# A graph network layer: gathered rows as float16 high and low parts that TensorE adds to the products, and 47 double groups, not 18, fetched row by row

## The chip, the cores and the metric

The kernel runs on one core of one Trainium2 chip. That core has five engines with a queue of instructions each: TensorE (PE in the profile, its weight loads PEld), VectorE (DVE), ScalarE (ACT), GpSimd (POOL) and SyncE (SP). The queues run in order and wait for each other only through semaphores. The metric is the device time of one execution in microseconds (us). Before the change it is 3845.28 us, the median of three runs (3842.6 to 3846.54).

## What is computed

One layer of message passing over 12500 nodes with 128 features and 400000 edges, sorted by their target `dst`. Cut to what matters:

```
h   = relu(layernorm(x))                          # 12500 x 128
m   = relu(concat(h[src], h[dst], ea) @ w1 + b1) @ w2 + b2      # 400000 edges
agg = segment_sum(m, dst)
gi, gh = agg @ w_ih + b_ih, h @ w_hh + b_hh        # GRU gates
r, z = sigmoid(i_r + h_r), sigmoid(i_z + h_z);  n = tanh(i_n + r * h_n)
out = x + (1 - z) * n + z * h
```

`w1` has three parts: 128 rows for the source node, 128 for the target, 32 for the edge's own attributes. So the term of the source is a row of A = h @ w1[0:128], which is computed once per node and then fetched once per edge. Those 400000 fetches of 512 bytes, at addresses that only `src` tells, are what this change is about.

## The kernel before

**Tiling.** The edges make 3125 tiles of 128. Eight tiles are a double group (a pair k, 391 of them, the first with fewer tiles), and a pair is worked on in two halves u = 2k and 2k + 1 of four tiles (782 halves). The edges of a pair have targets in a short window of nodes. A tile has its edges on the 128 partitions; in a half, the four tiles lie beside each other, 128 x 512 numbers.

**Prologue.** The nodes are loaded in 25 chunks of up to four tiles; layer norm; a transpose on PE into `hT_all`, which holds h for all nodes with the features on the partitions and stays in SBUF; then A = h @ w1a, copied out of PSUM into `asb` by ScalarE in every fourth chunk and by VectorE in the others (L304), and written to DRAM. POOL begins to gather at once: the first ten pairs (`RAW`) take rows of x, not of A, and are normalised and multiplied tile by tile.

**A pair in the main loop.** `gather` (L135 to L146) issues eight indirect DMAs on POOL, one per tile, into a buffer G. There are two rings: eight buffers (`GBUFS`), and four more (`EARLY`) for the first pairs, which are closed later to make room for the jobs below. `fetch` (L483, L486) loads the edge attributes and the targets of two pairs into L and Ld over SP; L has three buffers. `onehot_T` (L493, VectorE) makes the upper rows of L a one-hot matrix of the target within the window, `onehot` (L542) the same with edges on the partitions. `window` (L512, L515) copies the window's columns of `hT_all` and multiplies them by w1b on PE; `window_rows` (L524) adds b1 and puts the result into RW over the attribute's part of w1. With that, one matmul of L by RW (L590) gives the sum of the target's and the attribute's terms for two tiles.

**A half.** `pre` (L586 to L602) issues two such matmuls into a PSUM tile (two of these exist); `add` (L605 to L615, VectorE) adds the gathered rows of A, from PSUM and G into G; `relu` (L617 to L623, ScalarE) writes the result to RB; `seg` (L625 to L636, PE) multiplies the one-hot matrix by it and so sums the edges per target. After a pair `take` copies the sums out (`sums` on VectorE, `dcol` on ScalarE). After every 14 pairs `node` computes the gates for the finished nodes, one step of it per half, spread over the queues.

**Pairs fetched by hand.** Some pairs don't use POOL. `one_by_one` (L762 to L781) loads 32 indices at a time into registers (L768) and then moves, edge by edge, a column of `hT_all` into a tile HE, as four bytes per partition: ScalarE with a copy (L775), VectorE with a maximum over one element (L777). Such a pair has 1024 edges. HE holds columns of h, so in `pre` PE multiplies each of its eight tiles by w1a into the same PSUM tile (L601), there is nothing to add, and `relu` reads PSUM. Ten pairs go to ScalarE and eight to VectorE (`SPREAD`), at even distances. A job is cut into steps of four edges (`STEP`), and `run_jobs` spreads its steps over the halves between the previous job's end and four halves before its pair is due, in four phases per half.

**The order.** It is written out by hand. In half u, phase 0 of the jobs comes first, then `take` of the pair before, then `stages(u)` (one-hots for three pairs ahead, `pre` for half u + 3, `add` and `relu` for u + 2), phase 1 and `window`, phase 2, `seg(u)`, phase 3 and `window_rows`, and a step of the node work. `JOBS0` (16) is the pair at which the jobs begin.

Of the kernel before, what the change touches and what calls it, by code (L numbers as in the profile page):

```python
# [37 lines left out]
NFULL = N // 128  # L38
BAT = (4,) + (8,) * 11 + (NFULL - 92, 1)
RAW = 10  # L40
GBUFS = 8
EARLY = 4
PLACE = 20
CH = PLACE * PAIR
LOAD = 32
STEP = {"act": 4, "dve": 4}
SPREAD = {"act": 10, "dve": 8}
NR = 12672

H_AT = 16512  # L50
HOLD = -2


@with_exitstack
def tile_gnn(ctx: ExitStack, tc: tile.TileContext, x, src, srcT, dstT, dstP, eaT, eaP, w1, b1, w2T, b2,
# [50 lines left out]
    def dst_tile(c):  # L106
        if c >= NPL:
# [4 lines left out]

    ident = const.tile([128, 128], F32, name="ident")
    make_identity(nc, ident)
    iota = const.tile([128, V], F16, name="iota")
    nc.gpsimd.iota(iota, pattern=[[1, V]], base=0, channel_multiplier=0,
                   allow_small_or_imprecise_dtypes=True)
    A = dram.tile([N, D], F32, name="A")
    stats = dram.tile([N, 2], F32, name="stats")
    S = dram.tile([NR, D + 1], F32, name="S")  # L120

# [13 lines left out]
    def gather(k):  # L135
        if k >= NP or k in mode:
            return
        pool = ge if early_pair(k) else gp
        G[k] = pool.tile([128, GRP, 2, D], F32, name="G")
        table = x if k < RAW else A  # L140
        for u in (2 * k, 2 * k + 1):
            for t, j, a in unit_tiles(u):
                c, i = divmod(t, CH)
                nc.gpsimd.indirect_dma_start(  # L144
                    out=G[k][:, j, a, :], out_offset=None, in_=table,
                    in_offset=bass.IndirectOffsetOnAxis(ap=src_i[c][:, i:i + 1], axis=0))  # L146

    for k in range(RAW):
# [59 lines left out]
    with tc.tile_pool(name="pp", bufs=3) as pp:  # L208
# [69 lines left out]
        def chunk(q):  # L278
            b, c = chunks[q]
            i0, n = bats[b]  # L280
            return b, i0, c, min(n, c + 4), PB(b), (i0 + c) * 128
# [3 lines left out]
        for q in range(NC + 3):  # L285
            if q < NC:
                b, i0, c, e, P, n0 = chunk(q)
                if c == 0:
                    stat(b + 2)
                    fin(b + 1)  # L290
            if 1 <= q <= NC:
                b, i0, c, e, P, n0 = chunk(q - 1)
                pts[q - 1] = ps2.tile([128, 512], F32, name="oh")
                for j in range(c, e):
                    nc.tensor.transpose(pts[q - 1][:, (j - c) * P:(j - c + 1) * P],
                                        xs[b][:P, j, :], ident[:P, :P])
                if e == bats[b][1]:
                    load(b + 5)
            if q >= 3:
                b, i0, c, e, P, n0 = chunk(q - 3)  # L300
                if c == 0:
                    asb[b] = pp.tile([128, 8, D], F32, name="asb", bufs=2)
                copy = nc.scalar.copy if q % 4 == 2 else nc.vector.tensor_copy
                copy(asb[b][:P, c:e, :], pas.pop(q - 3)[:P, :e - c, :])  # L304
            if q < NC:
                b, i0, c, e, P, n0 = chunk(q)
                for j in range(c, e):
                    relu_norm(xs[b][:P, j, :], xs[b][:P, j, :], st_all[:P, i0 + j, :])
                if e == bats[b][1]:
                    sqr(b + 2)  # L310
            if 1 <= q <= NC:
                b, i0, c, e, P, n0 = chunk(q - 1)
                copy = nc.scalar.copy if q % 4 == 0 else nc.vector.tensor_copy
                copy(columns(b, c, e), pts.pop(q - 1)[:, :(e - c) * P].rearrange(
                    "f (i p) -> f i p", i=e - c))
            if q >= 3:
                b, i0, c, e, P, n0 = chunk(q - 3)
                if e == bats[b][1]:
                    nc.sync.dma_start(nodes(A, i0, e, P), asb[b][:P, :e, :])
            if 2 <= q <= NC + 1:  # L320
                b, i0, c, e, P, n0 = chunk(q - 2)
                pas[q - 2] = ps2.tile([128, GRP, D], F32, name="pre")
                for j in range(c, e):
                    nc.tensor.matmul(pas[q - 2][:P, j - c, :], columns(b, j, j + 1)[:, 0, :],
                                     w1a, start=True, stop=True)
# [145 lines left out]
        nc.vector.tensor_copy(flag, f[:, 6:7])  # L471


    Ls, Ds, OH, RT, HE, SEG = ({} for _ in range(6))
    hand = {}

    def fetch(q):
# [104 lines left out]
    def pre(u):  # L582
        if u >= NU:
            return
        k, h = divmod(u, 2)
        PP[u] = ps2.tile([128, GRP, D], F32, name="pre")  # L586
        for i in range(2):
            c0 = (k % QP) * 512 + (2 * h + i) * 128
            raw = u in HE or k in hand
            nc.tensor.matmul(PP[u][:, 2 * i:2 * i + 2, :], Ls[k // QP][:, c0:c0 + 128], RW[k % 4],  # L590
                             start=True, stop=not raw)
            if raw:
                l = unit_tiles(u)
                for n, (t, j, a) in enumerate(l):
                    if j % 2 == i:
                        if k in hand:
                            c = (a * GRP + j) * 128
                            cols = hand[k][:, c:c + 128]
                        else:
                            cols = HE[u][:, n * 128:(n + 1) * 128]  # L600
                        nc.tensor.matmul(PP[u][:, 2 * i + a, :], cols, w1a, start=False,  # L601
                                         stop=n + 1 == len(l) or l[n + 1][1] != j)  # L602


    def add(u):  # L605
        if u >= NU:
            return
        if u in HE or u // 2 in hand:
            RT[u] = PP.pop(u)
            HE.pop(u, None)  # L610
            if u % 2:
                hand.pop(u // 2, None)
        else:
            RT[u] = unit(u)
            nc.vector.tensor_tensor(RT[u], PP.pop(u), RT[u], op=ALU.add)  # L615

    def relu(u):  # L617
        if u >= NU:
            return
        o = RB[u % 3]  # L620
        nc.scalar.activation(o[:, :, :D], RT.pop(u), AF.Relu)  # L621
        if u % 2:
            G.pop(u // 2, None)  # L623

    def seg(u):  # L625
        k, h = divmod(u, 2)
# [123 lines left out]

    pj = []
    late = ExitStack()
    by_hand = order["act"] + order["dve"]
    NJ = len(by_hand)
    at = const.tile([NJ, PAIR * 128], I32, name="at")

    def job_indices(r):
# [2 lines left out]
            "(o e) -> o e", o=1))  # L760

    def one_by_one(m, k):  # L762
        et = {"act": ET.Activation, "dve": ET.DVE}[m]
        r = by_hand.index(k)
        hand[k] = pj[0].tile([128, PAIR * 128], F32, name=f"HE_{m}")
        he = hand[k].bitcast(U8)
        for e0 in range(0, PAIR * 128, LOAD):
            _, vals = nc.values_load_multi_w_load_instructions(  # L768
                at[r:r + 1, e0:e0 + LOAD], engines=[et], min_val=H_AT,
                max_val=H_AT + 4 * (N - 1),  # L770
                skip_runtime_bounds_check_because="src holds numbers of nodes")
            for i, v in enumerate(vals):
                e = e0 + i
                if m == "act":
                    nc.scalar.copy(he[:, e * 4:e * 4 + 4], h_bytes[:, bass.ds(v - H_AT, 4)])  # L775
                else:
                    nc.vector.tensor_reduce(he[:, e * 4:e * 4 + 4],  # L777
                                            h_bytes[:, bass.ds(v - H_AT, 4), None],
                                            AX.X, ALU.max)
                if i % STEP[m] == STEP[m] - 1:  # L780
                    yield  # L781

# [2 lines left out]
    for m, kl in order.items():  # L785
        start = 2 * JOBS0
        for k in kl:
            end = 2 * k - 4
            jobs.setdefault(start, []).append((m, k, end - start))
            start = end  # L790
    live = {}

    PH = 4
# [37 lines left out]
    def stages(u):  # L831
        if u + 7 >= 0:
            raw_stats(u + 7)
        if u + 6 >= 0:
            raw_fin(u + 6)
            raw_h(u + 6)
        if u % 2 == 0:
            onehot_T(u // 2 + 3)
            onehot(u // 2 + 3)
        if u + 4 >= 0:  # L840
            raw_turn(u + 4)
        if u + 3 >= 0:
            pre(u + 3)
        if u + 2 >= 0:
            add(u + 2)
            relu(u + 2)

    for u in range(-7, 0):
# [13 lines left out]
    for u in range(NU):  # L862
# [14 lines left out]
        for r in range(2 * u, min(2 * u + 2, NJ)):  # L877
            job_indices(r)
        if u == 2 * JOBS0 - 2:
            nc.vector.tensor_scalar(at, at, 4.0, float(H_AT), op0=ALU.mult, op1=ALU.add)  # L880

        def other(phase):
            run_jobs(u, phase)
# [47 lines left out]
    def general_edges(i, low, spare):  # L931
# [3 lines left out]
        nc.sync.dma_start(idst, dstT[:, bass.ds(i, 1)])  # L935
        ea = fb.tile([128, 128], F32, name="ea")
        nc.sync.dma_start(ea[64:96, :], eaT[:, bass.ds(i * 128, 128)])
        ag = fb.tile([128, D], F32, name="ag")
        rows_of(ag, A, isrc)
        xd = fb.tile([128, D], F32, name="xd")  # L940
        rows_of(xd, x, idst)
        sd = fb.tile([128, 2], F32, name="sd")
# [7 lines left out]
        nc.tensor.matmul(pn[:, :D], hT, w1b, start=True, stop=False)  # L950
        nc.tensor.matmul(pn[:, :D], ea[64:96, :], RW[0][64:96, 0, :], start=False, stop=True)
        R = fb.tile([128, D + 1], F32, name="R1")
        nc.vector.tensor_tensor(ag, ag, b1b, op=ALU.add)
        nc.vector.tensor_tensor(ag, ag, pn[:, :D], op=ALU.add)
        nc.scalar.activation(R[:, :D], ag, AF.Relu)
        nc.vector.memset(R[:, D:D + 1], 1.0)
# [117 lines left out]
```

## Time and profile before

| | |
|---|---|
| median of the runs | 3845.28 us |
| the profiled execution as a run | 3851.33 us |
| its span, first to last instruction | 3849.6 us |
| mean granted clock of PE | 0.752 of full speed |
| DMA, mean | 87 GB/s |
| first and last reduce by hand on VectorE | 241.6 and 3568.5 us |
| last gather, last relu | 3807.2 and 3810.6 us |

In the profile's groups, "x" is the number of instructions; then come the busy time and the mean in ns of one, and after the bar the idle time of the engine just before them, with what ended most of it. "Issue" means that nothing the profile shows was waited for. Records of PE count every matmul of float32 twice[...]. Instructions of one engine can overlap by their ends, so a group's busy time can be less than its number times the mean. Loads of registers and the issue of a DMA are not busy time; they are listed under the engine's queue (DVEq, ACTq, SPq).

### The profile page before, as it was taken

What the parts mean: (1) busy time and instruction counts of PE and PEld (TensorE: products, weight loads), DVE (VectorE), ACT (ScalarE), POOL (GpSimd) and SP (SyncE); (2) the same over time, 40 slices, a digit from 0 to 9 for tenths busy, and PEclk for the clock granted to TensorE, in tenths of its full rate; (3) what the DMA queues carried; (4) which work ended last, traced back from release to release, by engine and by line L of the source; (5) the groups of instructions that cost most, each with busy time, mean ns of one, the idle gap of its engine ahead of it and who ended that gap; (6) DMA issues with size and microseconds to landing.
All of it is one profiled execution on the core that took longest, in us unless ns stands there. A gap on an engine that the chain in (4) does not pass through costs nothing. (4 is left out here: it accounts for less than half of the span.)

```text
span 3849.6 us, 62154 instructions
## 1 busy us (share of the span) xinstructions
PE 2660.6 (69%) x13274; PEld 1624.1 (42%) x13274; DVE 2007.8 (52%) x12309; ACT 1650.1 (43%) x11720; POOL 2895.7 (75%) x2989
## 2 busy tenths in 40 slices
PE   6688766766775675776777577666667766775776
PEld 6554443443443443443444344433434443443443
DVE  7766655544545444554555455455545545544432
ACT  5446544444444444443544444444444444444311
POOL 7777777777777777777777777777777777777774
PEclk9888777777777777776777787687867777777776
DMA  6343333333333333333333333333333333333331
GB/s 202 87 99 93 85 91 84 77 87 82 88 82 87 82 84 85 84 86 79 90 84 83 81 88 87 77 92 78 89 80 89 77 87 82 89 80 85 88 81 38
DMA packets 151695, 333.68 MB, mean 87 GB/s; under 512 B 62088, under 2 KB 68019, under 8 KB 151317
## 3 DMA queue, kind: packets, MB, share of 16 engines
q0 software_dynamic: 95392, 195.55, 20.1%
q1 hardware_dynamic: 55781, 134.06, 13.5%
q8 instruction: 110, 1.80, 0.2%
q14 instruction: 268, 2.20, 0.2%
q10 hardware_dynamic: 144, 0.07, 0.0%
HBM read 315.60 MB, written 13.84 MB: 86 GB/s over the span
## 5 line engine op out<-in xcount | busy, mean ns | idle before, releaser
L144 POOL DMA_INDIRECT G<-A,src_i x2904 | 2821.9, 972 | 886.8 <-issue 837.3
L590 PE MATMUL pre<-RW,L 128*128 128x256 f32 x3128 | 1164.7, 505 | 120.4 <-DVE G L615 107.5
L775 ACT COPY HE_act<-hT_all 128x4 uint8 x10240 | 1055.5, 188 | 380.8 <-issue 378.9
L621 ACT ACTIVATE RB<-G 128x512 f32<-128x512 f32 x726 | 456.9, 629 | 1409.2 <-DVE G L615 1099.0
L615 DVE TENSOR_TENSOR G<-pre,G 128x512 f32<-128x512 f32 x726 | 499.8, 688 | 890.4 <-DMA G<-A,src_i 876.2
L515 PE MATMUL oh<-w1b,hw 128*64 128x128 f32 x782 | 217.1, 370 | 1019.8 <-DVE hw L512 1014.0
L590 PEld LDWEIGHTS pre<-RW,L 128*128 128x128 f32 x3128 | 696.7, 246 | 435.2 <-issue 311.3
L777 DVE TENSOR_REDUCE HE_dve<-hT_all 128x4 uint8 x8192 | 641.3, 148 | 359.8 <-issue 354.2
L634 PE MATMUL seg<-RB,OH 128*32 128x129 f32 x6250 | 657.4, 346 | 6.0 <-ACT dcol L643 4.4
L515 PEld LDWEIGHTS oh<-w1b,hw 128*64 128x64 f32 x782 | 92.6, 168 | 1184.2 <-DVE hw L512 1154.0
L634 PEld LDWEIGHTS seg<-RB,OH 128*32 128x32 f32 x6250 | 356.3, 133 | 256.6 <-issue 139.9
L524 DVE TENSOR_TENSOR RW<-oh,b1b 32x128 f32<-32x128 f32 x782 | 218.9, 280 | 171.8 <-PE oh L515 164.8
L642 DVE COPY sums<-seg 64x128 f32<-64x128 f32 x391 | 108.5, 278 | 211.0 <-PE seg L634 207.1
L493 DVE TENSOR_SCALAR L<-Ld,node_of 64x512 f32<-64x512 int32 x391 | 193.9, 496 | 0.1
L643 ACT CAST dcol<-seg 64x1 f16<-64x1 f32 x391 | 59.6, 152 | 261.2 <-DVE sums L642 259.0
L665 PEld LDWEIGHTS nd<-spot,sums 64*128 64x128 f32 x782 | 164.4, 321 | 13.8 <-issue 13.8
L665 PE MATMUL nd<-spot,sums 64*128 64x40 f32 x782 | 168.5, 404 | 0.0
L542 DVE TENSOR_TENSOR OH<-dloc,iota 128x256 f32<-128x256 f16 (+1 forms) x392 | 160.0, 408 | 0.0
L629 PE MATMUL seg<-zrow 1*64 1x129 bf16 x391 | 107.1, 274 | 0.0
L512 DVE COPY hw<-hT_all 128x64 f32 x391 | 85.3, 218 | 18.2 <-issue 7.0
L144 POOL DMA_INDIRECT G<-in_x,src_i x77 | 72.8, 946 | 24.9 <-issue 22.8
L629 PEld LDWEIGHTS <-zrow 1*64 1x64 bf16 x391 | 43.6, 111 | 97.4 <-issue 97.4
(147 smaller groups left out, 1366.4 us busy)
## 6 DMA issues: line engine op xcount, KB each, us to landing
L<-in_eaP SPq DMA_DIRECT2D x195, 256.0 KB
Ld<-in_dstP SPq DMA_DIRECT2D x390, 128.0 KB
G<-A,src_i POOLq DMA_INDIRECT x2904
xb<-in_x SPq DMA_DIRECT2D x28, 256.0 KB
out<-xb SPq DMA_DIRECT2D x28, 256.0 KB
xs<-in_x SPq DMA_DIRECT2D x11, 512.0 KB
A<-asb SPq DMA_DIRECT2D x11, 512.0 KB
src_i<-in_srcT SPq DMA_DIRECT2D x19, 80.0 KB
```

Of the source, the lines that this page charges most:

```text
L144: nc.gpsimd.indirect_dma_start(out=G[k][:, j, a, :], out_offset=None, in_=table, in_offset=bass.IndirectOffsetOnAxis(ap=src_i[c][:, i:i + ...
L493: nc.vector.tensor_scalar(Ls[k // QP][:2 * V, c], Ds[k // QP][:, c], node_of[:, k:k + 1], None, op0=ALU.is_equal)
L515: nc.tensor.matmul(PB_[k][:2 * V, :D], hw.rearrange("p a v -> p (a v)"), w1b, start=True, stop=True)
L524: nc.vector.tensor_tensor(RW[k % 4][s, a, :], pm[s, :D], b1b[s, :], op=ALU.add)
L542: nc.vector.tensor_tensor(o, d.to_broadcast(shape), i.to_broadcast(shape), op=ALU.is_equal)
L590: nc.tensor.matmul(PP[u][:, 2 * i:2 * i + 2, :], Ls[k // QP][:, c0:c0 + 128], RW[k % 4], start=True, stop=not raw)
L615: nc.vector.tensor_tensor(RT[u], PP.pop(u), RT[u], op=ALU.add)
L621: nc.scalar.activation(o[:, :, :D], RT.pop(u), AF.Relu)
L634: nc.tensor.matmul(SEG[k][V * a:V * (a + 1), :D + 1], OH[k][:, j, a, :], RB[u % 3][:, (j % 2) * 2 + a, :D + 1], start=False, stop=all(b != ...
L665: nc.tensor.matmul(pt[:, bass.ds(offs[i], V + SHIFT)], sums[:, i, :], spot, start=False, stop=i == n - 1)
L775: nc.scalar.copy(he[:, e * 4:e * 4 + 4], h_bytes[:, bass.ds(v - H_AT, 4)])
L777: nc.vector.tensor_reduce(he[:, e * 4:e * 4 + 4], h_bytes[:, bass.ds(v - H_AT, 4), None], AX.X, ALU.max)
```

## The change

A is written as two float16 parts: `hi` is 16 a rounded to float16, `lo` is what is missing, 16 a - hi. A row still has 512 bytes. In `pre`, PE multiplies both parts of the gathered rows by a diagonal matrix `unscale` of 1/16 and accumulates them in the PSUM tile with the product of L and RW. `add` is gone, and `relu` always reads PSUM.

ScalarE gets 19 pairs by hand and VectorE 22. A third kind of job is new: six pairs whose rows SP fetches from A, one DMA of 512 bytes per edge, with the address in a register, two edges per step; these end eight halves before their pair is due, and the next begins at the half after it. Their rows lie as gathered ones do, in a buffer of their own. The indices in `at` are scaled for each kind. The ring of gather buffers has seven, not eight, and the jobs begin at pair 15. `onehot` moves from the even to the odd halves. The branch for inputs whose windows don't fit, which these inputs don't take, adds both parts up by itself.

```diff
-GBUFS = 8
+GBUFS = 7
-STEP = {"act": 4, "dve": 4}
-SPREAD = {"act": 10, "dve": 8}
+STEP = {"act": 4, "dve": 4, "sp": 2}
+SPREAD = {"act": 19, "dve": 22, "sp": 6}
+SCALE = 16.0
+ROW = 512
...
+    unscale = const.tile([128, 128], F16, name="unscale")
+    nc.vector.tensor_scalar(unscale, ident, 1.0 / SCALE, None, op0=ALU.mult)
-    A = dram.tile([N, D], F32, name="A")
+    A = dram.tile([N, 2 * D], F16, name="A")
...
-                copy = nc.scalar.copy if q % 4 == 2 else nc.vector.tensor_copy
-                copy(asb[b][:P, c:e, :], pas.pop(q - 3)[:P, :e - c, :])
+                hi, lo = asb[b][:P, c:e, :D], asb[b][:P, c:e, D:]
+                pa = pas.pop(q - 3)[:P, :e - c, :]
+                nc.scalar.activation(hi, pa, AF.Copy, scale=SCALE)
...
+                nc.vector.scalar_tensor_tensor(lo, pa, SCALE, hi, op0=ALU.mult,
+                                               op1=ALU.subtract)
...
         PP[u] = ps2.tile([128, GRP, D], F32, name="pre")
+        raw = u in HE or k in hand
+        if not raw:
+            parts = unit(u).bitcast(F16)
+            for i in range(2):
+                nc.tensor.matmul(PP[u], unscale, parts[:, :, i * D:(i + 1) * D],
+                                 start=i == 0, stop=False)
...
-                             start=True, stop=not raw)
+                             start=raw, stop=not raw and i == 1)
...
-    def add(u):
...
-            nc.vector.tensor_tensor(RT[u], PP.pop(u), RT[u], op=ALU.add)
...
-        nc.scalar.activation(o[:, :, :D], RT.pop(u), AF.Relu)
+        nc.scalar.activation(o[:, :, :D], PP.pop(u), AF.Relu)
...
     def one_by_one(m, k):
+        if m == "sp":
+            G[k] = pj[0].tile([128, GRP, 2, D], F32, name="G_sp", bufs=1)
+            rows = G[k].bitcast(U8)
...
+                else:
+                    a, j = divmod(e // 128, GRP)
+                    nc.sync.dma_start(rows[e % 128:e % 128 + 1, j, a, :],
+                                      A_bytes[bass.ds(v, ROW)].rearrange("(o f) -> o f", o=1))
...
-            end = 2 * k - 4
+            end = 2 * k - (8 if m == "sp" else 4)
             jobs.setdefault(start, []).append((m, k, end - start))
-            start = end
+            start = end if m != "sp" else 2 * k + 2
...
         if u % 2 == 0:
             onehot_T(u // 2 + 3)
+        elif u > -7:
             onehot(u // 2 + 3)
...
-            add(u + 2)
             relu(u + 2)
...
-            nc.vector.tensor_scalar(at, at, 4.0, float(H_AT), op0=ALU.mult, op1=ALU.add)
+            nc.vector.tensor_scalar(at, at, place_of[:, 0:1], place_of[:, 1:2],
+                                    op0=ALU.mult, op1=ALU.add)
```

More of the change, by code (lines that the diff above doesn't have):

```diff
@@ L140, in gather @@
         table = x if k < RAW else A
+        rows = G[k] if k < RAW else G[k].bitcast(F16)
         for u in (2 * k, 2 * k + 1):
@@ L144, in gather @@
                 nc.gpsimd.indirect_dma_start(
-                    out=G[k][:, j, a, :], out_offset=None, in_=table,
+                    out=rows[:, j, a, :], out_offset=None, in_=table,
                     in_offset=bass.IndirectOffsetOnAxis(ap=src_i[c][:, i:i + 1], axis=0))
@@ L301, in tile_gnn @@
                 if c == 0:
-                    asb[b] = pp.tile([128, 8, D], F32, name="asb", bufs=2)
-                copy = nc.scalar.copy if q % 4 == 2 else nc.vector.tensor_copy
-                copy(asb[b][:P, c:e, :], pas.pop(q - 3)[:P, :e - c, :])
+                    asb[b] = pp.tile([128, 8, 2 * D], F16, name="asb", bufs=2)
+                hi, lo = asb[b][:P, c:e, :D], asb[b][:P, c:e, D:]
+                pa = pas.pop(q - 3)[:P, :e - c, :]
+                nc.scalar.activation(hi, pa, AF.Copy, scale=SCALE)
             if q < NC:
@@ L471, in check_windows @@
         nc.vector.tensor_copy(flag, f[:, 6:7])
-    Ls, Ds, OH, RT, HE, SEG = ({} for _ in range(6))
+    Ls, Ds, OH, HE, SEG = ({} for _ in range(5))
     hand = {}
@@ L586, in pre @@
         PP[u] = ps2.tile([128, GRP, D], F32, name="pre")
+        raw = u in HE or k in hand
[4 more added lines that the diff above has]
+                                 start=i == 0, stop=False)
         for i in range(2):
             c0 = (k % QP) * 512 + (2 * h + i) * 128
-            raw = u in HE or k in hand
             nc.tensor.matmul(PP[u][:, 2 * i:2 * i + 2, :], Ls[k // QP][:, c0:c0 + 128], RW[k % 4],
-                             start=True, stop=not raw)
+                             start=raw, stop=not raw and i == 1)
             if raw:
@@ L602, in pre @@
                                          stop=n + 1 == len(l) or l[n + 1][1] != j)
-    def add(u):
[L606 to L615, printed above, removed]
     def relu(u):
@@ L620, in relu @@
         o = RB[u % 3]
-        nc.scalar.activation(o[:, :, :D], RT.pop(u), AF.Relu)
+        nc.scalar.activation(o[:, :, :D], PP.pop(u), AF.Relu)
+        HE.pop(u, None)
         if u % 2:
             G.pop(u // 2, None)
+            hand.pop(u // 2, None)
     def seg(u):
@@ L752, in tile_gnn @@
     late = ExitStack()
-    by_hand = order["act"] + order["dve"]
+    by_hand = [k for m in ("sp", "act", "dve") for k in order[m]]
     NJ = len(by_hand)
+    NSP = len(order["sp"])
+    place_of = const.tile([NJ, 2], F32, name="place_of")
+    for i, (to_sp, to_others) in enumerate(((ROW, 4), (0, H_AT))):
+        nc.vector.memset(place_of[:, i:i + 1], float(to_others))
+        nc.vector.memset(place_of[:NSP, i:i + 1], float(to_sp))
+    A_bytes = A.bitcast(U8).rearrange("n f -> (n f)")
     at = const.tile([NJ, PAIR * 128], I32, name="at")
@@ L762, in one_by_one @@
     def one_by_one(m, k):
-        et = {"act": ET.Activation, "dve": ET.DVE}[m]
+        et = {"act": ET.Activation, "dve": ET.DVE, "sp": ET.SP}[m]
         r = by_hand.index(k)
-        hand[k] = pj[0].tile([128, PAIR * 128], F32, name=f"HE_{m}")
-        he = hand[k].bitcast(U8)
+        if m == "sp":
+            G[k] = pj[0].tile([128, GRP, 2, D], F32, name="G_sp", bufs=1)
+            rows = G[k].bitcast(U8)
+        else:
+            hand[k] = pj[0].tile([128, PAIR * 128], F32, name=f"HE_{m}")
+            he = hand[k].bitcast(U8)
         for e0 in range(0, PAIR * 128, LOAD):
+            low, high = (0, ROW * (N - 1)) if m == "sp" else (H_AT, H_AT + 4 * (N - 1))
             _, vals = nc.values_load_multi_w_load_instructions(
-                at[r:r + 1, e0:e0 + LOAD], engines=[et], min_val=H_AT,
-                max_val=H_AT + 4 * (N - 1),
+                at[r:r + 1, e0:e0 + LOAD], engines=[et], min_val=low, max_val=high,
                 skip_runtime_bounds_check_because="src holds numbers of nodes")
@@ L775, in one_by_one @@
                     nc.scalar.copy(he[:, e * 4:e * 4 + 4], h_bytes[:, bass.ds(v - H_AT, 4)])
-                else:
+                elif m == "dve":
                     nc.vector.tensor_reduce(he[:, e * 4:e * 4 + 4],
@@ L779, in one_by_one @@
                                             AX.X, ALU.max)
+                else:
+                    a, j = divmod(e // 128, GRP)
+                    nc.sync.dma_start(rows[e % 128:e % 128 + 1, j, a, :],
+                                      A_bytes[bass.ds(v, ROW)].rearrange("(o f) -> o f", o=1))
                 if i % STEP[m] == STEP[m] - 1:
@@ L937, in general_edges @@
         nc.sync.dma_start(ea[64:96, :], eaT[:, bass.ds(i * 128, 128)])
-        ag = fb.tile([128, D], F32, name="ag")
-        rows_of(ag, A, isrc)
+        parts = fb.tile([128, 2 * D], F16, name="parts")
+        rows_of(parts, A, isrc)
         xd = fb.tile([128, D], F32, name="xd")
@@ L952, in general_edges @@
         R = fb.tile([128, D + 1], F32, name="R1")
-        nc.vector.tensor_tensor(ag, ag, b1b, op=ALU.add)
+        ag = fb.tile([128, D], F32, name="ag")
+        nc.vector.tensor_tensor(ag, parts[:, :D], parts[:, D:], op=ALU.add)
+        nc.vector.scalar_tensor_tensor(ag, ag, 1.0 / SCALE, b1b, op0=ALU.mult, op1=ALU.add)
         nc.vector.tensor_tensor(ag, ag, pn[:, :D], op=ALU.add)
```

## The prediction

> **What bounds the kernel now.** I read the table of busy times and the costliest groups first, then the stretches in time, then single instructions.
>
> ```profile
> PE 2660.6 (69%) x13274; PEld 1624.1 (42%) x13274; DVE 2007.8 (52%) x12309; ACT 1650.1 (43%) x11720; POOL 2895.7 (75%) x2989
> ...
> L144 POOL DMA_INDIRECT G<-A,src_i x2904 | 2821.9, 972 | 886.8 <-issue 837.3
> ...
> L775 ACT COPY HE_act<-hT_all 128x4 uint8 x10240 | 1055.5, 188 | 380.8 <-issue 378.9
> ...
> L615 DVE TENSOR_TENSOR G<-pre,G 128x512 f32<-128x512 f32 x726 | 499.8, 688 | 890.4 <-DMA G<-A,src_i 876.2
> ...
> L777 DVE TENSOR_REDUCE HE_dve<-hT_all 128x4 uint8 x8192 | 641.3, 148 | 359.8 <-issue 354.2
> ...
> L524 DVE TENSOR_TENSOR RW<-oh,b1b 32x128 f32<-32x128 f32 x782 | 218.9, 280 | 171.8 <-PE oh L515 164.8
> ...
> L642 DVE COPY sums<-seg 64x128 f32<-64x128 f32 x391 | 108.5, 278 | 211.0 <-PE seg L634 207.1
> ```
>
> POOL's 75% hides a full queue: 2904 gathers cost 2821.9 busy and 886.8 idle, nearly all of it "issue", so 1.277 us each; with the 77 from x (97.7 us) that is 3806 of the span's 3849.6. VectorE's add waits 876 us for the gathers. POOL is the bound.
>
> ```profile
> core 0: us, PE busy (x) PEld busy (x) DVE busy (x) ACT busy (x) POOL busy (x), PEclk, DMA share, GB/s
> 240.00:300.00 60.00, 50.45 (x256) 28.15 (x254) 44.86 (x315) 40.85 (x310) 45.98 (x47) 0.86 0.38 94
> ```
>
> In this stretch the gathers are still ahead. 18 adds (by group) fall in it, 3.3 us per half group, against 4.9 later (726 adds and 56 direct relus, 782 halves, in 3.8 ms). That is the pace when POOL does not bind, and PE's clock is 0.86, not the mean 0.752.
>
> **The change, part by part.** Reference: this execution, span 3849.6 (3851.3 as a run); the median of the runs is 6 lower.
>
> *Gathers.* The built program has 2672 + 77 of them, 232 fewer: 232 x 1.277 = 296 us off POOL. The ring loses a buffer, so pair 11, not pair 12, has to wait for pair 0, whose rows PE reads at about 121 us: some 12 us of idle. POOL alone then allows 3849.6 - 296 + 12 = **3565**.
>
> *VectorE.* The add goes (500 us). Hand groups rise from 8 to 22: 22528 reduces and 704 register loads. Their price:
>
> ```profile
> 1007.50 0.85 DVE L777 TENSOR_REDUCE HE_dve<-hT_all 128x4 uint8 x12
> ...
> 1014.15 0.58 DVE L524 TENSOR_TENSOR RW<-oh,b1b 32x128 f32<-32x128 f32 x2 [1.91 <-PE oh L515]
> ...
> 1016.39 0.35 DVE L777 TENSOR_REDUCE HE_dve<-hT_all 128x4 uint8 x4 [1.67 <-issue]
> ...
> 1018.15 1.60 ACT L775 COPY HE_act<-hT_all 128x4 uint8 x16
> ```
> ```profile
> L768 ACTq TENSOR_LOAD <-at x320: 1957/1969/2304, 242.8 to 3610.0; - x160
> L768 DVEq TENSOR_LOAD <-at x256: 2101/2151/2548, 239.4 to 3553.3; - x128
> ```
>
> Twelve reduces in 0.85 us, the last lasting 0.148: (0.85 - 0.148) / 11 = 0.064 each. A load of 32 indices holds the queue 2.15 us, of which 354.2 / 256 = 1.38 is seen as idle; the rest passes under instructions already handed over. A group: 1024 x 0.064 + 32 x 1.38 = 110 us. The idle is the disputed number. With nothing handed over it is 2.15 (+542 us over 704 loads); with more work ahead it might be 1.2 (-127). The removed add was part of the cover, but the bursts are twice as long (two steps of four per phase), and the row is hand work too: I take 1.38.
> Hand work runs from half group 30 to 756, 363 pairs. 22 x 110 = 2413. The rest of a pair: L493 0.496, L542 0.409, L512 0.218, L524 2 x 0.280, L642 0.278, and per pair 0.45 of node and placing work, less 0.3 because each starts before the last ends: 2.1, x 363 = 762. Together 3175.
> Stalls: `sums`, RW and TOT wait 207 + 165 + 113 us for PE today. With VectorE itself late PE is ahead; I leave 0.2 us a pair for L524 and 2 us a block for TOT: 130 (bounds 50 and 485). So 3305 us, 9.10 a pair, 4.55 a half, against POOL's 316 gathered pairs x 8 x 1.277 = 3228. **VectorE becomes the bound by a little.**
>
> *ScalarE.* Sixteen copies in 1.60: 0.094 each; a load 378.9 / 320 = 1.18. A group 134 us, x 19 = 2546. Relu reads PSUM (586 ns against 629), plus dcol and gates: 1.46 a pair, 530. Sum 3076, 8.5 a pair: below VectorE, not by much.
>
> *PE.* 1360 matmuls of 128x512 float16 come (two per gathered half), each with a load of `unscale`, and 29 more groups go through w1a (29.2 us busy per 10 groups): 85 us. The nearest row is the bf16 matmul of as many columns:
>
> ```profile
> L667 PE MATMUL misc<-zrow x28: 604/604/604, 232.7 to 3818.7; 1*128 1x512 bf16 x28
> ```
>
> That row says 604 ns. The Trainium skill ("TensorE: Matmul & The Clock Gate", part 1, the HAM clock gate) says that back-to-back such matmuls start 427 ns apart at the half clock a little-used PE gets, 216 at the full one. By the row 821 us, by the rule 581 or 294. Even by the row PE comes to 2660 + 85 + 821 = 3566, under 3725 but with no slack; the clock column (0.86 where PE is pressed) speaks for the rule, and the row is a whole latency, not a spacing. I take about 400, hidden beside VectorE. If that cover is gone, PE ends in VectorE's place near 3700.
>
> *Prologue.* Each of 25 chunks takes one ScalarE and one VectorE instruction (0.6 and 0.7) where there was one copy: some 15 us. It hides: the loop's start waits for `place_c`, which stands on POOL behind 77 gathers (13.3 us of VectorE idle before L364). The move of `onehot` to the odd half moves 0.4 us and nothing waits for it.
>
> *SP.* 6 x 1024 row transfers and 192 loads are issued in order with L and Ld.
>
> ```profile
> 133.78 1.45 SPq L759 DMA_DIRECT2D at<-in_src  x5
> ```
>
> One-partition transfers with fixed addresses start (1.45 / 5) 0.29 apart; a register address adds a move. No row shows it: 0.29 below, 0.45 above, I take 0.33. The Trainium skill ("DMA: Bandwidth & Descriptors", anatomy of one DMA) speaks against 512-byte transfers: some 2.0 us fixed each. Each of these waits for the one eight before: by the rule 2.0 / 8 = 0.25, below the row, so issue decides unless the latency passes 2.6 us. In sequence, at 2.0 us each, 6144 would be 12 ms.
> First job, halves 30 to 110: 1024 x 0.33 + 32 x 2.0 + 20 fetches x 1.55 + 15 of waits = 448, against 80 x 4.55 = 364. L's three buffers let SP lead by four halves and lag two: 27 us. It is late by **57 us**, and behind it L and Ld, so VectorE's one-hot (L493) waits. The later jobs have about 110 halves, 500 us, for some 465: free.
>
> *Sum.* 240 until the hand work starts (the first reduce is at 241.6) + 3305 + 57 + the end: 26 halves at 3.3 and 40 from the last relu (3810.6) to the end of the span, 126. 3728 of span; 2 more outside it and 6 less for the median: **3725 us**, 3.1% faster.
>
> **Rivals.**
> 1. *POOL stays the bound*: the loads hide better, SP is on time. For it: only 77 us between POOL's 3228 and VectorE's 3305. Against it: no engine has slack then. 3565 plus little: **3580**.
> 2. *SP sets the pace* (slower). L and Ld stand behind rows; if a row costs 0.45, the first job is late by 180 and five others by 61 each: 3671 + 485 = **4155**. At 0.40 it is level with before; that is the deciding point. For it: the L issue with 64 rows takes 0.47, the 512-byte cost with a register address is unseen. Against: the 0.29.
> 3. *VectorE's loads or waits are worse* (slower). At 1.55 us of idle per load (x 704, +120) the gain is gone; the instances above show 1.67 after a wait. With 1.7: **3950**. Against it: the mean of 256 loads is 1.38.
>
> That the groups do not come by hand is excluded: the counts above are those of the built program.
>
> **How the numbers follow.** Forecast 45%, own range 3660 to 3800. Rival 1 25%. Rival 3 15%, rival 2 11%, PE or ScalarE holding at about 3850 4%. Range 3580 to 3920: left out are the far end of rivals 2 and 3 (14%) and under 3580 (6%). Faster by over 0.2% (about what a measurement of this kernel tells from no change): the forecast and rival 1, 70%; within it 5%; slower 25%.
>
> **What would show it.** POOL: 2749 gathers, and idle beyond "issue", ended by PE. L791's idle over 704 loads: 1.38 right, over 1.55 rival 3. VectorE over 85% busy plus load idle between 250 and 3600. The row transfers' spacing on SP, and L493 waiting for Ld in the first 350 us of hand work only. PEclk over 0.8. Wrong would be: L493 waiting for Ld throughout (rival 2), POOL's idle all issue (rival 1), or PE busy over 90% and waited for by `sums`.

## The result, and the profile after

The changed kernel takes **3799.14 us** (median of four runs, 3786.18 to 3801.7), the kernel before on the same chip 3843.94. The ratio is 0.9876 with a 95% interval of 0.9858 to 0.9894: 1.2% faster. The forecast was 3725 us, 3.1% faster; the time lies inside the range of 3580 to 3920. The profiled execution took 3786.18 us as a run, 13 less than the median, with a span of 3784.3; the forecast's sum for that span was 3728.

First the page of the kernel after, busy times and groups. The lines have moved: the gather is L150, the reduce L791, the one-hot L502, `window_rows` L533, `sums` L645; L600 is the matmul that adds the gathered rows.

```profile
PE 2764.6 (73%) x15002; PEld 1709.0 (45%) x15002; DVE 2470.6 (65%) x25930; ACT 2494.0 (66%) x20956; POOL 2627.9 (69%) x2757
...
L150 POOL DMA_INDIRECT G<-A,src_i x2672 | 2554.0, 956 | 1085.8 <-issue 747.1
...
L791 DVE TENSOR_REDUCE HE_dve<-hT_all 128x4 uint8 x22528 | 1602.0, 145 | 969.1 <-issue 961.9
...
L600 PE MATMUL pre<-G,unscale 128*128 128x512 f16 x1336 | 487.6, 453 | 48.4 <-ACT RB L622 46.2
...
L502 DVE TENSOR_SCALAR L<-Ld,node_of 64x512 f32<-64x512 int32 x391 | 191.2, 489 | 92.1 <-DMA Ld<-in_dstP 81.5
```

No engine is over 73% busy (before, none over 75%). But VectorE's 2470.6 and its 961.9 of load idle make 3432 of 3784. The waits show the other side, who waits for whom (total, times, longest in us):

```profile
PE oh L524 <- DVE hw L521: 898.2, 303, 16.1
...
POOL G L150 <- PE pre L600: 267.2, 54, 26.9
...
ACT dcol L646 <- DVE sums L645: 481.0, 309, 9.8
...
DVE L L502 <- DMA Ld<-in_dstP: 81.5, 15, 11.0
```

POOL, which never waited for a free buffer beyond the start before, now does so 54 times: its ring is full, and it is no longer the bound. PE and ScalarE wait for VectorE. PE's wait alone doesn't show that: before, when VectorE itself stood 876 us waiting for gathers, PE waited 1014.0 us for the same copy. What is new is that VectorE, beside its loads, waits for nothing longer than the 81.5 us above in sum. In its timeline (start, duration, instruction, idle before it) a pair in the middle looks so:

```profile
1002.18 0.60 DVE L791 TENSOR_REDUCE HE_dve<-hT_all 128x4 uint8 x8 [0.95 <-issue]
1002.70 0.41 DVE L551 TENSOR_TENSOR OH<-dloc,iota 128x256 f32<-128x256 f16 x1
1003.04 1.61 DVE L791 TENSOR_REDUCE HE_dve<-hT_all 128x4 uint8 x24
1004.57 0.68 DVE L720 TENSOR_TENSOR gt<-gt 128x512 f32<-128x512 f32 x1
1006.27 0.60 DVE L791 TENSOR_REDUCE HE_dve<-hT_all 128x4 uint8 x8 [1.02 <-issue]
1006.90 0.28 DVE L645 COPY sums<-seg 64x128 f32<-64x128 f32 x1
1007.11 0.47 DVE L502 TENSOR_SCALAR L<-Ld,node_of 64x512 f32<-64x512 int32 x1
```

Nothing but its own work and the "issue" before a reduce, where a load of 32 indices lies bare. So the middle goes at VectorE's pace.

The last line of the waits, L502's 81.5 us for Ld, belongs to one stretch. By stretches (busy time of each engine, count, then PE's clock):

```profile
core 0: us, PE busy (x) PEld busy (x) DVE busy (x) ACT busy (x) POOL busy (x), PEclk, DMA share, GB/s
300.00:700.00 400.00, 245.65 (x1251) 147.45 (x1252) 202.88 (x2202) 211.07 (x1827) 255.73 (x268) 0.75 0.29 76
1000.00:2000.00 1000.00, 743.50 (x3969) 449.84 (x3969) 675.95 (x7501) 705.65 (x6207) 713.36 (x749) 0.84 0.33 85
```

Between 300 and 700 us every engine is slower than later: VectorE is busy for 51% of the time instead of 68%, and POOL for 64%, not 71%. This is where SP's first job runs. Its timeline there, with the one-hot that waits for it:

```profile
486.06 3.42 SPq L796 DMA_DIRECT2D G_sp<-A  x11
489.59 0.48 SPq L492 DMA_DIRECT2D L<-in_eaP  x1
490.12 1.04 SPq L495 DMA_DIRECT2D Ld<-in_dstP  x2
491.26 7.36 SPq L796 DMA_DIRECT2D G_sp<-A  x18
```
```profile
494.79 0.48 DVE L502 TENSOR_SCALAR L<-Ld,node_of 64x512 f32<-64x512 int32 x1 [5.91 <-DMA Ld<-in_dstP]
```

The rows follow each other on SP without a break, L and Ld stand in line behind them, and VectorE begins the one-hot 4.7 us after their issue (490.12 to 494.79), as soon as they land. Just before SP's job, at 215 us, the trace has Ld issued 17.4 us ahead of its use; six pairs on, at 278 us, it is 4.4, and it stays between 3.9 and 5.6 until the job ends at 686 us.

The pace, from the starts of the relus, in us per half:

| kernel | halves 50 to 110 | halves 120 to 710 | median of the runs, us |
|---|---|---|---|
| before | 4.16 | 4.87 | 3843.94 |
| after | 5.85 | 4.65 | 3799.14 |

### The profile page after: what moved, and what is told of

Same layout as the page of the kernel before. It is cut to its first block, busy times and chain, and to the rows that moved or that the text cites. A ratio compares the mean times of both kernels' runs of the same rounds, so it can differ in the third digit from the quotient of the medians.

```text
span 3784.3 us, 99056 instructions
## 1 busy us (share of the span) xinstructions
PE 2764.6 (73%) x15002; PEld 1709.0 (45%) x15002; DVE 2470.6 (65%) x25930; ACT 2494.0 (66%) x20956; POOL 2627.9 (69%) x2757
## 4 chain that ended last, share of the span: by engine, by line
DVE 35%; PE 25%; issue 20%; SPq 12%; DMA 4%; DVEq 2%; POOL 2%; ACT 0%; ACTq 0%; POOLq 0%
DVE HE_dve L791 22%; SPq L796 8%; PE pre L604 5%; PE nd L668 3%; DMA Ld<-in_dstP 3%; PE seg L637 3%; DVE RW L533 3%; SPq L783 3%; DVE L L502 2%; PE pre L600 2%; POOL G L150 2%; DVEq L783 2%; DVE OH L551 2%; PE oh L524 1%; PE nd L687 1%
## 5 line engine op out<-in xcount | busy, mean ns | idle before, releaser
L150 POOL DMA_INDIRECT G<-A,src_i x2672 | 2554.0, 956 | 1085.8 <-issue 747.1
L789 ACT COPY HE_act<-hT_all 128x4 uint8 x19456 | 1967.8, 191 | 565.8 <-issue 563.0
L791 DVE TENSOR_REDUCE HE_dve<-hT_all 128x4 uint8 x22528 | 1602.0, 145 | 969.1 <-issue 961.9
L604 PE MATMUL pre<-RW,L 128*128 128x256 f32 x3128 | 986.4, 440 | 6.0 <-ACT RB L622 3.6
L524 PE MATMUL oh<-w1b,hw 128*64 128x128 f32 x782 | 190.1, 329 | 910.6 <-DVE hw L521 898.2
L604 PEld LDWEIGHTS pre<-RW,L 128*128 128x128 f32 x3128 | 692.3, 227 | 228.2 <-issue 68.8
L637 PE MATMUL seg<-RB,OH 128*32 128x129 f32 x6250 | 591.5, 319 | 0.0
L622 ACT ACTIVATE RB<-pre 128x512 f32<-128x512 f32 x782 | 460.8, 589 | 122.9 <-PE seg L637 122.3
L600 PE MATMUL pre<-G,unscale 128*128 128x512 f16 x1336 | 487.6, 453 | 48.4 <-ACT RB L622 46.2
L637 PEld LDWEIGHTS seg<-RB,OH 128*32 128x32 f32 x6250 | 327.0, 123 | 209.3 <-issue 159.1
L502 DVE TENSOR_SCALAR L<-Ld,node_of 64x512 f32<-64x512 int32 x391 | 191.2, 489 | 92.1 <-DMA Ld<-in_dstP 81.5
L533 DVE TENSOR_TENSOR RW<-oh,b1b 32x128 f32<-32x128 f32 x782 | 216.8, 277 | 52.5 <-PE oh L524 45.9
L600 PEld LDWEIGHTS <-unscale 128*128 128x128 f16 x1360 | 97.8, 102 | 247.3 <-issue 239.5
L551 DVE TENSOR_TENSOR OH<-dloc,iota 128x256 f32<-128x256 f16 (+1 forms) x392 | 162.5, 415 | 0.5 <-issue 0.2
L645 DVE COPY sums<-seg 64x128 f32<-64x128 f32 x391 | 109.8, 281 | 76.4 <-PE seg L637 67.3
L150 POOL DMA_INDIRECT G<-in_x,src_i x77 | 73.0, 947 | 24.9 <-issue 23.2
```

The source lines that it names most:

```text
L150: nc.gpsimd.indirect_dma_start(out=rows[:, j, a, :], out_offset=None, in_=table, in_offset=bass.IndirectOffsetOnAxis(ap=src_i[c][:, i:i + ...
L502: nc.vector.tensor_scalar(Ls[k // QP][:2 * V, c], Ds[k // QP][:, c], node_of[:, k:k + 1], None, op0=ALU.is_equal)
L524: nc.tensor.matmul(PB_[k][:2 * V, :D], hw.rearrange("p a v -> p (a v)"), w1b, start=True, stop=True)
L533: nc.vector.tensor_tensor(RW[k % 4][s, a, :], pm[s, :D], b1b[s, :], op=ALU.add)
L600: nc.tensor.matmul(PP[u], unscale, parts[:, :, i * D:(i + 1) * D], start=i == 0, stop=False)
L622: nc.scalar.activation(o[:, :, :D], PP.pop(u), AF.Relu)
```

## Experiments

The theory: VectorE's reduces and bare loads pace the middle (4.65 us a half), and SP's first job, which has 80 halves of time where the others have 108 to 112, stretches halves 30 to 110. Rivals: POOL is still the bound; SP sets the pace throughout; the loads' idle is off the path; PE's added matmuls are felt. The runs of this section stand against 3845.57 us (the first four) and 3841.26 us (the last four) of the kernel before on the same chip. Where POOL gets back a group it issues eight gathers more.

**No groups over SP.**

```diff
-SPREAD = {"act": 19, "dve": 22, "sp": 6}
+SPREAD = {"act": 19, "dve": 22, "sp": 0}
...
```

Here and in the run with PE's addition alone the kernel also leaves out the fill of SP's scale, since SP has no groups.

> The changed kernel with no groups over SyncE (6 groups back to POOL's gathers). Theory (VectorE paces the middle, SyncE only makes its first job late): the lateness of some 80 us goes, VectorE's 22 groups stay, so 3710 to 3730, with L502 no longer waiting for Ld and half groups 50 to 120 at about 4.65 us each. Rival POOL still bound: 48 gathers more x 1.28 = 61 us slower than the changed kernel, about 3860. Rival SyncE paces throughout: under 3660.

3705.51 us, ratio 0.9635 (0.9614 to 0.9656): POOL has 48 gathers more, and the kernel is 94 us faster than with SP's help. Halves 50 to 110 go at 4.44 us, the middle at 4.68, about as in the changed kernel, and L502 has no wait for Ld left. The time is 4 us below the expected 3710. POOL as the bound is refuted by the sign.

**SP's six groups kept, with equal windows.** The pairs are placed so that every job of SP has 110 to 116 halves.

```diff
-        lo = JOBS0 + 15
+        lo = JOBS0 + (0 if m == "sp" else 15)
-            k = lo + int((i + 0.5) * (NP - 2 - lo) / n)
+            k = lo + int((i + (0.95 if m == "sp" else 0.5)) * (NP - 2 - lo) / n)
```

> The changed kernel with SyncE's six groups kept, but placed so that each has 110 to 116 half groups of time, the first too (it had 80). Theory (only the first job's window is too short): 3710 to 3730, the waits of L502 for Ld almost gone. Rival (the rows on SyncE cost wherever they stand): as the changed kernel, 3790 to 3810. Rival (the early stretch is slow for other reasons, such as ScalarE or PE starting its groups there): also 3790 or more, with other waits in half groups 50 to 120.

3698.43 us, ratio 0.9619 (0.9603 to 0.9635), 12 below the expected 3710. The same 6144 rows cost nothing now. The waits of VectorE between 245 and 720 us, and the stretches, in this kernel:

```profile
DVE HE_dve L791 <- issue: 137.7, 97, 2.2
...
DVE L L502 <- DMA Ld<-in_dstP: 1.8, 2, 1.0
```
```profile
300.00:700.00 400.00, 305.51 (x1604) 184.78 (x1602) 264.02 (x2893) 274.84 (x2400) 303.29 (x318) 0.83 0.35 89
1000.00:2000.00 1000.00, 741.74 (x3996) 450.81 (x3998) 677.20 (x7456) 701.38 (x6158) 709.77 (x743) 0.85 0.33 84
```

L502's wait has gone from 81.5 to 1.8 us, VectorE in the early stretch from 202.88 to 264.02 busy, and the middle is as it was. So the window was at fault: 93 us of span (3784.3 to 3690.9). It is a narrow thing even with 110 halves: the trace has Ld's lead down to 4.2 us once more, at 393 us, near half 70.

**Loads of 8 indices, not 32, for VectorE and ScalarE.**

```diff
-LOAD = 32
+LOAD = {"act": 8, "dve": 8, "sp": 32}
...
```

`LOAD[m]`, by the kind of job, stands where `LOAD` stood.

> The changed kernel with VectorE's and ScalarE's indices loaded 8 at a time instead of 32, so that less of a load lies bare behind the instructions handed over. Theory (the idle of loads is part of what paces VectorE; a load of 8 takes about 0.6 us, so most of it passes under the instructions before it): VectorE's load idle falls from 953 us to some 500 or less, middle pace from 4.65 to about 4.2 us a half group, 3500 to 3680, unless POOL (some 3570) or ScalarE takes over. Rival (another engine paces, the idle of loads is not on the path): unchanged, 3790 to 3810. Rival (each load costs its queue a fixed 1.4 us whatever its length): 2112 more loads on VectorE, over 4500.

3615.04 us, ratio 0.9397 (0.9379 to 0.9414). The groups, and the loads on VectorE's queue (min, median, max in ns):

```profile
L791 DVE TENSOR_REDUCE HE_dve<-hT_all 128x4 uint8 x22528 | 1724.9, 147 | 547.3 <-issue 515.5
L789 ACT COPY HE_act<-hT_all 128x4 uint8 x19456 | 1958.3, 192 | 16.1 <-issue 10.6
```
```profile
L783 DVEq TENSOR_LOAD <-at x2816: 591/604/1166, 230.1 to 3505.7; - x188
```

The idle falls from 961.9 to 515.5 us while the reduces' busy time rises by 123 (more of each lies open to the next load), so VectorE is freed of 323; the kernel gains 184. The pace of the middle is 4.38 a half, and POOL's own is about that: 316 gathered of 363 pairs, 8 x 1.26 us each, over two halves, gives 4.39. The idle of loads was on the path, up to where POOL takes over. SP's first job still costs its part (5.84 in halves 50 to 110).

**The hand groups alone: the kernel before with 19 and 22, VectorE still adding.**

```diff
-SPREAD = {"act": 10, "dve": 8}
+SPREAD = {"act": 19, "dve": 22}
```

> The kernel before with 19 and 22 hand groups instead of 10 and 8, none over SyncE, the addition left on VectorE. Theory (VectorE paces once it has 22 groups): POOL's 184 gathers fewer save at most 235 us, but VectorE holds 0.69 us of addition for each of about 680 gathered half groups beside its 4.65 us a half, so the middle goes at about 5.2 us a half: 4050 to 4200, slower than before. Rival (POOL still sets the end): 3615 to 3650, faster than the change itself.

4067.34 us, ratio 1.0566 (1.0538 to 1.0593): slower than before, with 184 gathers fewer. 5.20 us a half in the middle. Its groups and POOL's wait:

```profile
L615 DVE TENSOR_TENSOR G<-pre,G 128x512 f32<-128x512 f32 x680 | 464.5, 683 | 11.3 <-issue 1.2
```
```profile
POOL G L144 <- ACT RB L621: 515.7, 184, 16.7
```

The addition no longer waits for gathers (890.4 us before, now 11.3), and POOL waits for buffers instead. Moving work off POOL pays here only once VectorE is rid of the addition.

**PE's addition alone**, with 10 and 8 hand groups, the ring of 7 and nothing over SP.

```diff
-SPREAD = {"act": 19, "dve": 22, "sp": 6}
+SPREAD = {"act": 10, "dve": 8, "sp": 0}
...
```

> PE's addition alone: the float16 halves, the two matmuls of a gathered half group and the ring of 7, with 10 and 8 hand groups as before and nothing over SyncE. Theory (POOL is the bound before, and PE's added time is hidden): POOL's 2981 gathers stay, 12 us more for the ring: 3845 to 3865, PE's float16 matmul about 280 ns start to start. Rival (PE's 1360 more matmuls are felt): over 3900.

3813.94 us, ratio 0.9925 (0.9907 to 0.9944): 31 us below the expected 3845. PE's added time is hidden, and POOL is the bound as expected, but it has become quicker. The groups:

```profile
L150 POOL DMA_INDIRECT G<-A,src_i x2904 | 2781.5, 958 | 896.3 <-issue 787.7
...
L600 PE MATMUL pre<-G,unscale 128*128 128x512 f16 x1452 | 534.5, 456 | 928.1 <-DMA G<-A,src_i 767.5
L604 PE MATMUL pre<-RW,L 128*128 128x256 f32 x3128 | 1035.4, 461 | 3.6 <-ACT dcol L646 2.2
```

The mean of a gather is 958 ns, where it was 972; the last begins at 3776.3 us, not 3807.2. The traces don't put that down to the missing addition itself. The long gathers stand beside the one-hot with edges on the partitions (`onehot`): in the kernel before, the 375 gathers in whose first 0.9 us L542 ran took 1127 ns on average, the other 2529 took 949. Of the gathers beside neither one-hot, those beside an addition took 947 ns and those without one 948. With PE's addition, where `onehot` (now L551) stands in the odd half, the gathers beside it took 970 ns. Why it costs less there was not tested: the change moves the one-hot and drops the addition together.

**18 groups on VectorE, not 22.**

```diff
-SPREAD = {"act": 19, "dve": 22, "sp": 6}
+SPREAD = {"act": 19, "dve": 18, "sp": 6}
```

> The changed kernel with 18 groups on VectorE, not 22; 32 gathers go back to POOL. Theory (VectorE is the bound of the middle by about its own surplus over POOL): VectorE has 4 x 113 = 451 us less, POOL 41 more: POOL takes over at about 3565 + 41 = 3606, plus some of the first job's lateness on SyncE: 3610 to 3700. Rival (POOL is the bound): 3840. Rival (ScalarE or PE paces beside VectorE): 3790 to 3810.

3634.4 us, ratio 0.9459 (0.9439 to 0.9479): 165 us faster than the changed kernel, with 32 gathers more. The middle goes at 4.38 us a half, POOL's pace, and PE now waits for gathered rows:

```profile
L600 PE MATMUL pre<-G,unscale 128*128 128x512 f16 x1352 | 479.7, 442 | 321.7 <-DMA G<-A,src_i 189.8
```

VectorE had four groups too many for its long loads.

**Both corrections together: equal windows and loads of 8.** The edits are those two shown above.

> Both corrections in one: SyncE's six groups with equal windows, and VectorE's and ScalarE's indices loaded 8 at a time. Theory (VectorE paced the middle, and its two burdens were the load idle and the late first job): the loads took off 185 us and the windows 100; together at most 285, to some 3515, but POOL's 2749 gathers x 1.277 and its 43 us of start and ring allow no less than some 3560, so 3540 to 3590, with POOL's idle nearly all issue and VectorE waiting for G. Rival (the two overlap, both hide the same 100 us): about 3615, as with the small loads alone.

3525.08 us, ratio 0.9173 (0.9157 to 0.919), below the expected 3540: the two gains are separate (101 and 184 us alone, 274 together, where POOL is the bound). POOL's waits are those of an engine that never stops:

```profile
POOL G L150 <- issue: 755.2, 2477, 0.3
POOL G L150 <- DMA G<-A,src_i: 54.0, 177, 0.3
POOL G L150 <- PE misc L584: 12.5, 2, 12.2
```

No wait for a buffer is longer than 0.3 us, but for the 12.2 at the start, which the prediction had as the price of the smaller ring. 2749 gathers in 3485 us are 1.268 each, not the 1.277 that the expectation took; that is 25 us. At this pace SP's first job (492 us) fills its 110 halves: Ld's lead falls to 4.4 us again, and VectorE waits 11.7 us for Ld there.

**The same with 25 groups on ScalarE, 22 on VectorE and 5 over SP.**

```diff
-SPREAD = {"act": 19, "dve": 22, "sp": 6}
+SPREAD = {"act": 25, "dve": 22, "sp": 5}
```

> The same with 25 groups on ScalarE, 22 on VectorE and 5 over SyncE: 40 gathers fewer on POOL. Theory (POOL is the bound of the combined kernel): 40 x 1.277 = 51 us less than that, 3490 to 3540. Rival (VectorE or ScalarE is already the bound again): no gain, or slower by the 97 us a group that ScalarE gets more, up to 3650.

**3482.13 us, ratio 0.9056 (0.9035 to 0.9077)**, 9.4% faster than before, against 1.2% for the change as it was made, and 8 below the expected 3490. The 40 gathers bring 43 us, where 51 were expected. POOL still waits for a buffer only at the start, and ScalarE, at 87%, has used most of its slack:

```profile
PE 2670.6 (77%) x15074; PEld 1674.4 (48%) x15074; DVE 2615.3 (75%) x25930; ACT 3044.0 (87%) x27100; POOL 2602.8 (75%) x2717
```

**Four of these on another chip.** The first four runs were on a chip on which the kernel before itself took 5375.43 us; the expected times don't apply there, so these runs can't test the theories and are given for completeness. No groups over SP:

> The six groups that SP fetched go back to POOL (48 gathers, 61 us more for POOL, whose own sum is then about 3625). Theory (VectorE is the bound, SP only in its first job): VectorE's work is unchanged, L502's waits for Ld (92 us, all before 720 us) go, so about 3700 to 3720. Rival, SP paces the whole run: nearer to POOL's sum, about 3640. Rival, POOL is still the bound: slower than after by up to 61 us, about 3850.

5235.02 us, ratio 0.974 (0.9716 to 0.9763). 18 groups on VectorE:

> Four groups leave VectorE for POOL: VectorE loses 4 x 113 = 450 us of work, POOL gains 32 gathers (41 us, its sum about 3605). Theory: VectorE stops binding, the first SP job still costs some 80 us, so about 3650 to 3700. Rival, SP paces the whole run: unchanged within 20 us. Rival, POOL binds: about 40 us slower.

5411.95, ratio 1.0074 (1.0044 to 1.0105). Loads of 8:

> VectorE and ScalarE load 8 indices at a time instead of 32 (SP keeps 32). If a load's time goes with the number of values (0.31 us for one, 2.12 for 32), one of 8 takes about 0.75, and what is already handed to the engine covers nearly all of it. Theory: VectorE's idle of 962 us falls below 400 and the time to about 3650 to 3680, where POOL and the first SP job remain. Rival, the idle is not on the path: unchanged. Rival, a load has a fixed price: four times as many loads make it slower by 1000 us or more.

5574.43, ratio 1.0367 (1.0337 to 1.0398). PE's addition alone:

> Only A's two parts, the add on PE and the ring of seven, with the 10 and 8 groups by hand of before and none on SP. POOL's 2981 gathers stay: theory: the time of before plus about 12 us for the ring, 3840 to 3865. Rival, the matmuls on PE bind or PE's waits for ScalarE do: slower than 3900.

4908.6, ratio 0.9121 (0.9098 to 0.9143). The ratios rise with the number of instructions in the trace (62032, 86619, 94781 and 102992), but the kernel before, with 62154, stands at 1, so their number alone doesn't tell the time. The group of reduces in the run with 18 groups:

```profile
L791 DVE TENSOR_REDUCE HE_dve<-hT_all 128x4 uint8 x18432 | 1455.4, 147 | 1617.4 <-issue 1607.4
```

A reduce takes its usual 147 ns; the idle before it is twice the 808.5 us of the same kernel above. What held the instructions back there was not found out.

## Why the prediction was right and wrong

**Right: the direction, and that VectorE becomes the bound.** POOL waits for buffers for 267 us (rival 1 falls, and so it does with the run without SP's groups, which has more gathers and is faster). The idle of a load is 961.9 / 704 = 1.37 us, where 1.38 was taken and 1.55 would have cost the gain (rival 3 falls). The rest of a pair on VectorE is 2.09 us in the trace, 2.1 in the sum. All instructions and the load idle fill 93% of VectorE's time from 245 to 3500 us. PE's clock in the hand stage is 0.84, over 0.8 as said.

**What failed: two terms of the sum were too small**, VectorE's 3305 us and SP's 57 us. The starts of the relus divide the span as the prediction did (the relu of half u + 2 is issued in half u):

| part of the span, us | taken | measured | difference |
|---|---|---|---|
| until the hand work | 240 | 232.5 | -8 |
| its 726 halves with SP on time (measured with equal windows) | 3305 | 3360.6 | +56 |
| SP's first job late (3454.4 - 3360.6) | 57 | 93.8 | +37 |
| the end | 126 | 97.4 | -29 |
| span | 3728 | 3784.3 | +56 |

The other 18 of the 74 us missed are the profiled execution, which lies 13 below the median where the one before lay 6 above.

**The first failed step: a reduce at 0.064 us.** The spacing inside a burst is right (1.61 us for 24: (1.61 - 0.145) / 23 = 0.064), but before each of the 704 loads stands a last reduce whose 0.145 nothing covers. The prediction took that tail out of its row, (0.85 - 0.148) / 11, and didn't put it back. From the start of a reduce to the next instruction or to its own end it is 67.2 ns on average: 22528 x 3.2 ns = 72 us, more than the whole 56. This is read from the trace; no run changes it alone. What gave the remainder back isn't told apart.

**The second: "It is late by 57 us", SP's first job.** Place and mechanism were right: VectorE's waits for Ld are in the first 450 us of the hand work (350 were said) and nowhere else. The size was not: giving the job a wider window brings 93 us of span, and 101 of the median. All three parts of 448 - 364 - 27 were off by about as much. The job lasted 462 us. With equal windows its 80 halves took 352. And L's three buffers did not give 27 us of lead: the trace shows 17.4 at the job's start, which shrinks to the 4.4 of landing, so 13. 462 - 352 - 13 = 97, against the 94 measured. The rows themselves were well priced, 0.323 us from start to start, 0.33 in the sum. On SP's queue:

```profile
L796 SPq MOVE G_sp<-A x6144: 29/29/38, 223.3 to 3457.3; - x199
L796 SPq DMA_DIRECT2D G_sp<-A x6144: 224/228/307, 223.3 to 3457.3; - x199
```

The Trainium skill's fixed 2.0 us per DMA ("DMA: Bandwidth & Descriptors", anatomy of one DMA) is given there for DMAs that POOL issues, so for SP's rows it was only a hint. Latency didn't set their pace, as the prediction judged: in the trace each row waits on the semaphore of the one eight before it, and they still start 0.323 us apart. Rival 2, SP as the pace of all jobs, had the right mechanism and the wrong reach: at 0.323 the five later jobs fit into their windows.

With SP's job on time the kernel takes 3698, 3.8% off. So the forecast's main claim stood: VectorE as the bound by a little. One short window took most of the gain away. The time came as near to 3725 as it did because both ends of the span were overpriced by some 37 us together, which was luck.

**PE** was taken to gain 485 us of busy time and gained 104. Of the 485, 85 were for 29 more groups through w1a; it is 23 (41 by hand for 18), since SP's rows lie as gathered ones, so about 67. The matmuls that were there became shorter, with the mean clock going from 0.752 to 0.846. Before and after:

```profile
L590 PE MATMUL pre<-RW,L 128*128 128x256 f32 x3128 | 1164.7, 505 | 120.4 <-DVE G L615 107.5
...
L604 PE MATMUL pre<-RW,L 128*128 128x256 f32 x3128 | 986.4, 440 | 6.0 <-ACT RB L622 3.6
```

By the clock alone 505 ns would become 505 x 0.752 / 0.846 = 449. The rule that the prediction weighed (the Trainium skill, "TensorE: Matmul & The Clock Gate", part 1: the clock follows how busy PE has been) agrees in direction: PE was 69% busy at 0.752, 73% at 0.846, and 77% at 0.879 in the fastest run. No run here changes PE's work alone. That the clock might rise and make the old matmuls shorter was left out of the sum. PE's time was hidden, so none of the span hung on it.

## What to carry to other kernels

When a queue carries both a background job and the loads of the main loop, compare the job's length with its own window for every job, the first above all, and measure how far the loads run ahead at that moment instead of counting buffers. Compare again when something else makes the kernel faster, since every window shrinks with the pace. When work moves to the next engine, move what frees that engine first (the addition), and stop at the number of groups where the two are level: 19 and 22 groups made the kernel 5.7% slower without it. A load into registers that lies bare behind short instructions is a bound of its own; cut it until the instructions before it cover it.

## What the runs showed that was not expected

- A load of indices into registers costs by its length: 2.125 us for 32 values and 0.604 for 8 on VectorE's queue. Four short ones take longer than one long one, and still only half as much is left bare.
- PE's 1452 float16 matmuls of 512 columns, 534.5 us of busy time, raised PE's whole busy time by only 110 (2660.6 to 2771.0 with PE's addition alone), while the granted clock went from 0.752 to 0.83. That fits L604's mean: 505 x 0.752 / 0.83 = 458 ns by the clock, 461 measured.
- Gathers on POOL became 14 ns shorter on average with PE's addition (972 to 958), and the last began 31 us earlier. Away from the one-hots, additions beside them had cost nothing (947 ns with, 948 without); beside the one-hot L542 they took 1127 ns against 949. What shortened them is open.
